# Strassen's scheme for one product of a four-layer graph network, with its norms put off and its Sturm counts taken from both ends

## The chip, the cores and the metric

The kernel runs on one core of one Trainium2 chip. The metric is the device time of the program in microseconds (us). Before the change it was 2614.92 us, the median of three runs (2614.4 to 2616.12).

## The reference

`x` is 128 graphs of 64 nodes with 256 features: 8192 rows of 256, all in fp32, and `adj` is one 64x64 matrix. Four layers follow each other, and each computes `x = layernorm(x + layer(x))`. Cut to what matters:

```python
# layer 0
A2 = adj * adj
h = relu(A2 @ (x @ W1))          # 256 -> 512
h = relu(A2 @ (h @ W2))          # 512 -> 1024
y = A2 @ (h @ W3)                # 1024 -> 256
# layer 1
L = normalized_laplacian(adj); _, U = eigh(L)
y = U @ (relu((U.T @ x) @ W1 + b1) @ W2 + b2)
# layer 2: two graph convolutions, then LSTMs over windows of 1, 2, 3, 4 nodes
# layer 3: graph attention
```

Layer 0 and the eigenvectors of one 64x64 matrix do not depend on each other; layer 1 needs both.

## The kernel before

The rows stand as 64 tiles of 128 (two graphs each) in `X` in SBUF for the whole run. There are two stages.

**Stage one** is layer 0 and, beside it, the eigenvectors. `layer0(g)` is a generator that works on 256 rows (two tiles) in five steps. `mixed` multiplies by the squared adjacency (`sqT2`, two graphs in one 128x128 block), which also brings the features onto the partitions; the product with W1 gives `h1`; `mixed` again gives `m2` (512 features in 4 chunks by 256 rows); the second product takes `m2` through W2 (`aw2`), 8 chunks of outputs with 4 matmuls of 128x256 each, and ScalarE (ACT) applies relu from PSUM into `h2`; the third product with W3 and a last product with `sqT2` give the layer's output. VectorE adds it to `X` (line 658) and `norm_parts` normalises (lines 472 to 485: statistics on VectorE, the power on GpSimd, the scaling on VectorE).

`eigen` is a second generator. It takes the 64x64 matrix to tridiagonal form in 62 steps (lines 140 to 196). Each step is one small matmul `pc` on TensorE (line 75) and some 25 small VectorE instructions on 64 partitions, of which line 163 writes the operand `LV` of the next matmul. Then Sturm counts find all 64 eigenvalues at once (lines 288 to 310): 6 passes with 16 trial points for each; each pass walks the 64 rows with a reciprocal and a multiply-add per row (lines 298 and 299), each depending on the one before. The rest (lines 313 to 454) makes the eigenvectors from recursions and transposes.

A planner puts the streams in order. It keeps `now`, a TensorE clock that each `mm` advances by a fixed cost, and each generator yields the time from which it may go on. The planner takes the first stream that is due, with `eigen` ahead of two groups of layer 0 (line 668 and following). `eigen` yields `after(n)`, which adds 0.21 us for each of n VectorE instructions to its own clock. In this stage TensorE and VectorE run their instructions exactly in the order in which the generators emit them (`manual_schedule`). PSUM is shared as 5 banks for layer 0 (`ps`) and 3 for `eigen` (`pa`, `pb`, `pc`).

**Stage two** is layers 1 to 3 on 16 groups of 512 rows, three groups in flight (`WAYS`), with a planner of its own for TensorE. `layer1` starts each group with `mixed` from `X`. The LSTM weights `wih` are loaded at the start of the kernel, `whh` when the first stage's pools close.

## Time and profile before

| | us |
|---|---|
| median of the runs | 2614.92 |
| profiled execution, own time | 2613.84 |
| its span | 2612.0 |
| TensorE busy | 2554.1 |
| VectorE busy | 1401.1 |
| ScalarE busy | 1048.5 |
| layer 0's last matmul starts | 923.51 |
| second stage's first matmul with X | 924.70 |
| last `LV` copy of the tridiagonal steps | 443.2 |
| first and last start of line 291 (Sturm passes) | 464.1, 690.1 |

The span is the time from the first to the last instruction in the trace; the execution's own time is 1.8 us longer. A row of the profile's groups names the line, the engine, the operation, what is written and read, the shape and the number; then the busy time, the mean of one in ns, and the idle time of that engine just before, with what ended it. A fp32 matmul is two instructions in the trace, so 64 rows of "128x256" are 32 matmuls of the source.

### The profile page before, as it was taken

The page shows a single profiled execution, that of the slowest core. Times are in us where ns is not written, and L with a number is a line of the kernel's source. Part 1 is how long each engine was busy: PE and PEld are TensorE (multiplying, and loading weights), DVE is VectorE, ACT ScalarE, POOL GpSimd, SP SyncE. Part 2 cuts the span into 40 slices and gives each one's busy share as a digit, 9 for nine tenths or more (in the row PEclk, how much of TensorE's full clock was granted, in tenths as well). Part 3 has the DMA queues.
Part 4 walks back from the last instruction along what each step waited for, and adds up shares of the span by engine and source line. Part 5 has one row for each costly group of instructions (what it writes and reads, how often), then busy time and mean ns, then how long its engine had stood idle before and what let it go on. Part 6 is the DMA issues. An engine that isn't in the chain of part 4 may idle for free.

```text
span 2612.0 us, 39806 instructions
## 1 busy us (share of the span) xinstructions
PE 2554.1 (98%) x15276; PEld 2240.8 (86%) x15276; DVE 1401.1 (54%) x5423; ACT 1048.5 (40%) x2599; POOL 132.2 (5%) x284
## 2 busy tenths in 40 slices
PE   8999999999999999999999999999999999999996
PEld 7888887888887889898899899898898998978994
DVE  5777777888864053434534544445445345353335
ACT  2232222222222234444544444544544444444444
POOL 0000000000000010000000000000000000000001
PEclk9999999999999999999999999999999999999998
DMA  8000000000000010000000000000000000000000
GB/s 278 1 1 1 1 1 1 1 1 1 1 1 1 1 49 1 9 1 9 9 1 9 9 1 9 7 4 9 1 9 9 1 9 9 1 9 1 1 2 25
DMA packets 24814, 32.19 MB, mean 12 GB/s; under 512 B 2352, under 2 KB 21552, under 8 KB 24624
## 3 DMA queue, kind: packets, MB, share of 16 engines
q1 hardware_dynamic: 24384, 29.60, 3.3%
q8 instruction: 120, 1.97, 0.3%
q14 instruction: 70, 0.57, 0.1%
q10 hardware_dynamic: 240, 0.05, 0.0%
HBM read 21.25 MB, written 8.39 MB: 11 GB/s over the span
## 4 chain that ended last, share of the span: by engine, by line
PE 87%; DVE 7%; ACT 3%; POOL 2%; issue 1%; DMA 0%; ACTq 0%; POOLq 0%; DVEq 0%
PE ps L607 84%; POOL ln_rs L475 1%; PE ps L720 1%; DVE X L485 1%; DVE ln_st L472 1%; PE ps L934 1%; DVE X L884 1%; PE pc L75 1%; ACT gates L821 1%; POOL ln_rs L474 1%; DVE ln_mv L473 0%; ACT L821 0%; ACT L947 0%; ACT att L947 0%; ACT w L876 0%
## 5 line engine op out<-in xcount | busy, mean ns | idle before, releaser
L607 PE MATMUL ps<-w,wih 128*128 128x128 f32 (+2 forms) x4992 | 895.5, 319 | 1.7 <-DVE w L840 1.7
L607 PEld LDWEIGHTS ps<-w,wih 128*128 128x128 f32 x4992 | 764.5, 191 | 51.3 <-issue 8.4
L821 ACT ACTIVATE gates<-ps,cbi 128x128 f32<-128x128 f32 (+2 forms) x1248 | 498.0, 409 | 568.0 <-PE ps L607 561.9
L607 PE MATMUL ps<-hs,whh 128*128 128x128 f32 (+2 forms) x3072 | 541.8, 304 | 7.9 <-DVE hs L831 7.6
L607 PEld LDWEIGHTS ps<-hs,whh 128*128 128x128 f32 x3072 | 454.4, 191 | 36.1 <-DVE hs L831 11.9
L607 PE MATMUL ps<-m,aw 128*128 128x256 f32 x2048 | 452.3, 380 | 0.0
L607 PEld LDWEIGHTS ps<-m,aw 128*128 128x128 f32 x2048 | 385.2, 190 | 50.2 <-issue 0.8
L615 ACT ACTIVATE h<-ps 128x256 f32<-128x256 f32 (+1 forms) x320 | 135.9, 425 | 393.6 <-PE ps L607 393.2
L607 PE MATMUL ps<-aw,h 128*128 128x256 f32 x1024 | 228.8, 380 | 0.0
L607 PEld LDWEIGHTS ps<-aw,h 128*128 128x128 f32 x1024 | 193.4, 190 | 36.5 <-issue 12.4
L826 DVE TENSOR_TENSOR gates<-gates 128x128 f32<-128x128 f32 (+2 forms) x256 | 89.1, 348 | 238.7 <-ACT gates L821 238.7
L474 POOL TENSOR_SCALAR ln_rs<-ln_mv 128x2 f32<-128x2 f32 x128 | 35.1, 274 | 2444.8 <-DVE ln_mv L473 2364.7
L829 ACT ACTIVATE gates<-c 128x128 f32<-128x128 f32 (+2 forms) x288 | 98.2, 341 | 114.0 <-DVE c L828 92.2
L485 DVE TENSOR_SCALAR X<-X,ln_mv,ln_rs 128x256 f32<-128x256 f32 x248 | 91.5, 409 | 96.7 <-POOL ln_rs L475 96.6
L840 DVE TENSOR_TENSOR w<-gates 128x256 f32<-128x256 f32 (+2 forms) x160 | 59.8, 379 | 130.4 <-PE ps L607 84.7
L825 DVE TENSOR_TENSOR c<-c,gates 128x128 f32<-128x128 f32 (+2 forms) x192 | 62.6, 326 | 117.5 <-ACT gates L821 115.3
L607 PE MATMUL ps<-aw,m 128*128 128x512 f32 x256 | 120.8, 595 | 0.0
L831 DVE TENSOR_TENSOR hs<-gates 128x128 f32<-128x128 f32 (+2 forms) x192 | 62.7, 328 | 101.9 <-ACT gates L829 52.9
L472 DVE BATCH_NORM_STATS2 ln_st<-X 128x6 f32<-128x256 f32 x256 | 99.0, 410 | 1.5
L298 DVE RECIPROCAL br<-Q 64x16 f32<-64x16 f32 x378 | 92.3, 244 | 12.5
L299 DVE SCALAR_TENSOR_TENSOR Q<-br,es,Q 64x16 f32<-64x16 f32 x378 | 85.8, 227 | 13.3
L475 POOL TENSOR_TENSOR ln_rs<-ln_rs,half 128x2 f32<-128x2 f32 x128 | 91.6, 716 | 10.0
(328 smaller groups left out, 2437.1 us busy)
## 6 DMA issues: line engine op xcount, KB each, us to landing
out_dram<-X SPq DMA_DIRECT2D x32, 256.0 KB, 2.1
X<-in_x_dram SPq DMA_DIRECT2D x31, 256.0 KB, 6.0
wih<-in_c_ih_dram SPq DMA_DIRECT2D x4, 1024.0 KB, 9.1
aw<-in_a_w_dram SPq DMA_DIRECT2D x3, 1024.0 KB, 9.9
whh<-in_c_hh_dram SPq DMA_DIRECT2D x3, 1024.0 KB, 5.5
aw<-in_a_w_dram SPq DMA_DIRECT2D x1, 512.0 KB, 4.6
cw<-in_c_w_dram SPq DMA_DIRECT2D x2, 256.0 KB, 3.5
X<-in_x_dram SPq DMA_DIRECT2D x2, 128.0 KB, 2.5
```

The source lines that it names most:

```text
L298: V.reciprocal(r, Q[:, k - 1, :])
L299: V.scalar_tensor_tensor(Q[:, k, :], r, es[:, 0, k:k + 1], Q[:, k, :], op0=ALU.mult, op1=ALU.add)
L472: nc.vector.bn_stats(st[:, t, :], x[:, t, :])
L475: nc.gpsimd.tensor_tensor(rs, rs, half[:, :n], ALU.pow)
L485: nc.vector.tensor_scalar(x[:, t, :], x[:, t, :], mv[:, t, 0:1], rs[:, t:t + 1], op0=ALU.subtract, op1=ALU.mult)
L607: PE.matmul(out, lhsT, rhs, start=start, stop=stop)
L615: S.activation(dst, src, AF.Relu)
L821: S.activation(gate[q][:, h, :], pp, AF.Tanh if q == "g" else AF.Sigmoid, bias=bias[:, j:j + 1])
L825: V.tensor_mul(c[:, h, :], c[:, h, :], gate["f"][:, h, :])
L826: V.tensor_mul(to, gate["i"][:, h, :], gate["g"][:, h, :])
L829: S.activation(gate["i"][:, h, :], c[:, h, :] if p > 1 else to, AF.Tanh)
L831: V.tensor_mul(new[:, h, :], gate["o"][:, h, :], gate["i"][:, h, :])
```

## The change

Layer 0 works on groups of 512 rows. Its second product is cut into 2x2 blocks: rows into two halves of 256, the 512 inputs into two halves, and the 1024 outputs into two halves. Winograd's form of Strassen's scheme makes the four blocks of the result with seven block products instead of eight. Four sums of blocks of `m2` (S1 to S4) are made on VectorE for every group, four sums of blocks of W2 (T1 to T4) once, in group 0. Each product is made in two parts (`j`), one PSUM bank each, and VectorE combines them (`u2`, `u3`, `join`), with relu on ACT from SBUF to SBUF afterwards.

The buffers of layer 0 become single (`pa` has bufs=1), groups wait for each other by name (`behind`), and PSUM is shared as 2 banks `ps`, 4 banks `prod`, 2 banks for `eigen` (`pb` is merged into `pa`). Only groups 0 to 2 are normalised in stage one; for the others, `group(g)` in stage two emits the norm ahead of `layer1`. `wih` is loaded when stage one closes, in turn with `whh`.

In `eigen`, the tridiagonal step loses one instruction: the small constant that line 151 added now stands in an extra column of `xr`. A step's due time is `after(30)` instead of `after(28)`. The Sturm counts run on 128 partitions: the lower 64 hold the matrix from its top, the upper 64 from its bottom, each half walks 32 rows, and the two join in the middle.

The diff, cut to its core:

```diff
     for i in range(N - 2):
-        V.tensor_scalar(rm, rest, 1e-30, None, op0=ALU.add)
-        V.tensor_scalar(ss, v0, v0, rm, op0=ALU.mult, op1=ALU.add)
+        V.tensor_scalar(ss, v0, v0, rest, op0=ALU.mult, op1=ALU.add)
...
-        yield after(28)
+        yield after(30)
...
+    HALF = N // 2
...
     for _ in range(PASSES):
...
-        for k in range(1, N):
-            r = sb([N, FAN], "br")
+        for k in range(1, HALF):
+            r = sb([W, FAN], "br")
             V.reciprocal(r, Q[:, k - 1, :])
-            V.scalar_tensor_tensor(Q[:, k, :], r, es[:, 0, k:k + 1], Q[:, k, :], op0=ALU.mult, op1=ALU.add)
+            V.scalar_tensor_tensor(Q[:, k, :], r, es2[:, k:k + 1], Q[:, k, :], op0=ALU.mult, op1=ALU.add)
             if k % 2:
                 yield after(7)
+        r = sb([W, FAN], "br")
+        V.reciprocal(r[:N, :], Q[:N, HALF - 1, :])
+        V.tensor_scalar(r[N:, :], r[:N, :], es[:, 0, HALF:HALF + 1], None, op0=ALU.mult)
+        V.tensor_add(Q[N:, HALF - 1, :], Q[N:, HALF - 1, :], r[N:, :])
...
-    pa = phase_a.enter_context(tc.tile_pool(name="pa", bufs=2))
+    pa = phase_a.enter_context(tc.tile_pool(name="pa", bufs=1))
...
-    wih = [load(keep, f"wih{i}", c_ih[i], "(k p) f -> p k f", [P, 2, 1024], p=P) for i in range(4)]
...
+    def behind(name, g):
+        while done[name] < g:
+            yield now[0] + 0.3
+
     def layer0(g):
-        xs = X[:, 2 * g:2 * g + 2, :]
+        xs = X[:, 4 * g:4 * g + 4, :]
...
+        if g == 0:
+            V.tensor_sub(T3, B22, B12)
+            V.tensor_sub(T1, B12, B11)
+            V.tensor_sub(T2, B22, T1)
+            V.tensor_sub(T4, T2, B21)
+        yield from behind("second", g - 1)
+        m2 = tl(pa, [P, 4, 512], "m2")
+        yield from mixed(m2, h1, 4, 1.4)
...
+        V.tensor_add(S1, A21, A22)
+        V.tensor_sub(S2, S1, A11)
+        V.tensor_sub(S3, A11, A21)
+        V.tensor_sub(S4, A12, S2)
...
-        for c in range(8):
-            p = tl(psa, [P, 512], "ps")
-            run(p[:, :2 * P], [(aw2[:, k, c * P:(c + 1) * P], m2[:, k, :]) for k in range(4)])
-            relu(h2[:, c, :], p[:, :2 * P])
-            yield now[0] + (1.3 if c == 7 else 0.0)
+        def product(w, a, j):
+            p = tl(psa, [P, 2, 256], "prod", bufs=4)
+            for i in range(2):
+                cols = slice((2 * j + i) * P, (2 * j + i + 1) * P)
+                run(p[:, i, :], [(w[:, k, cols], a[:, k, :]) for k in range(2)])
+            return p
...
+        def join(j, r, c, x, y, op=ALU.add):
+            V.tensor_tensor(quarter(j, r, c), x, y, op)
+            relu(quarter(j, r, c), quarter(j, r, c))
...
+            def six(p, p1=p1, u2=u2):
+                V.tensor_add(u2, p1, p)
+
+            def seven(p, u2=u2, u3=u3):
+                V.tensor_add(u3, u2, p)
+
+            def five(p, j=j, u2=u2, u3=u3):
+                join(j, 1, 1, u3, p)
+                V.tensor_add(u2, u2, p)
+
+            def four(p, j=j, u3=u3):
+                join(j, 1, 0, u3, p, ALU.subtract)
+
+            def three(p, j=j, u2=u2):
+                join(j, 0, 1, u2, p)
+
+            def two(p, j=j, p1=p1):
+                join(j, 0, 0, p1, p)
+
+            for then, w, a in ((one, B11, A11), (two, B21, A12), (six, T2, S2), (seven, T3, S3), (four, T4, A22),
+                               (five, T1, S1), (three, B22, S4)):
+                p = product(w, a, j)
+                if late:
+                    late[0](late[1])
+                late = then, p
...
                 yield now[0]
...
+        for t in (2, 0):
+            p = tl(psa, [P, 2, D], "ps", bufs=2)
+            mm(p, sqT2, s3[:, t:t + 2, :])
+            yield now[0] + 0.4
+            x2 = xs[:, t:t + 2, :]
+            V.tensor_add(x2, p, x2)
+            if g < WAYS:
+                rows_norm(tc, small, x2, half)
...
+    wih, whh = [], []
+    for i in range(4):
+        wih.append(load(wb, f"wih{i}", c_ih[i], "(k p) f -> p k f", [P, 2, 1024], p=P))
+        whh.append(load(wb, f"whh{i}", c_hh[i], "(k p) f -> p k f", [P, 2, 1024], p=P) if i else None)
...
     def group(g):
         xs = X[:, 4 * g:4 * g + 4, :]
-        ready = yield from layer1(xs)
+        ready = [0.0, 0.0]
+        if g >= WAYS:
+
+            ready = []
+            for t in range(0, 4, 2):
+                norm(xs, t, ready)
+        ready = yield from layer1(xs, ready)
```

The function that handles product `one` copies its bank to `p1` on ACT. Each product's additions are emitted after the next product's matmuls (`late`).

## The prediction

> **What bounds the kernel now.** I read the page's shares first, then the busy time of each engine by stage, then the timeline inside a stage. The page and its chain of waits say that TensorE sets the time:

> ```profile
> PE 2554.1 (98%) x15276; PEld 2240.8 (86%) x15276; DVE 1401.1 (54%) x5423; ACT 1048.5 (40%) x2599; POOL 132.2 (5%) x284
> ...
> PE 87%; DVE 7%; ACT 3%; POOL 2%; issue 1%; DMA 0%; ACTq 0%; POOLq 0%; DVEq 0%
> ```

> The 54% of VectorE is a mean over stages that differ. Busy time by stage, columns: stretch, its length, PE, PEld, DVE, ACT, POOL:

> ```profile
> 20.00:443.00 423.00, 419.19 (x2027) 347.69 (x2026) 324.60 (x1940) 123.13 (x373) 12.98 (x28) 1.00 0.09 29
> 443.00:464.00 21.00, 20.35 (x101) 16.01 (x100) 14.43 (x82) 4.95 (x12) 0.93 (x2) 1.00 0.00 1
> 464.00:738.00 274.00, 274.00 (x1289) 225.90 (x1288) 233.51 (x881) 70.00 (x168) 11.80 (x20) 1.00 0.00 1
> 738.00:812.00 74.00, 74.00 (x343) 60.47 (x342) 50.99 (x297) 17.25 (x42) 1.87 (x4) 1.00 0.00 1
> 812.00:924.50 112.50, 111.21 (x525) 91.05 (x524) 13.23 (x44) 27.56 (x66) 5.15 (x11) 1.00 0.06 20
> 924.50:2585.00 1660.50, 1630.28 (x10895) 1483.08 (x10893) 749.68 (x2121) 792.63 (x1911) 94.29 (x197) 1.00 0.02 6
> ```

> The rows are the tridiagonalisation, its clean-up, the Sturm counts, the rest of the eigenvectors, the end of layer 0, and the second stage. While the first four run, VectorE is busy 77%, 69%, 85% and 69% beside a full TensorE. That is the room into which the change puts additions. Timeline of one tridiagonal step (start, length, engine, line):

> ```profile
> 303.08 0.38 PE L75 MATMUL pc<-AQ,LV 128*128 128x128 f32 x2
> ...
> 303.50 0.23 DVE L175 SCALAR_TENSOR_TENSOR junk<-pc,q,xr 64x23 f32<-64x23 f32 x1 [1.88 <-PE pc L75]
> ...
> 305.02 0.14 DVE L151 TENSOR_SCALAR q<-q 64x1 f32<-64x1 f32 x1
> 305.20 0.26 DVE L152 TENSOR_SCALAR q<-xr,q 64x1 f32<-64x1 f32 x1
> ...
> 307.30 0.18 DVE L163 COPY LV<-u 64x64 f32<-64x64 f32 x1
> 307.41 0.67 DVE L658 TENSOR_TENSOR X<-ps,X 128x512 f32<-128x512 f32 x1
> ```

> From L175 to the end of L163 is 4.0 us, and L167 to L174 (300.28 to 301.61) came before it: 5.3 us of VectorE, in one piece, per step. 62 steps in 423 us are 6.8 us each. Two later rows:

> ```profile
> L298 DVE RECIPROCAL br<-Q 64x16 f32<-64x16 f32 x378 | 92.3, 244 | 12.5
> L299 DVE SCALAR_TENSOR_TENSOR Q<-br,es,Q 64x16 f32<-64x16 f32 x378 | 85.8, 227 | 13.3
> L658 DVE TENSOR_TENSOR X<-ps,X 128x512 f32<-128x512 f32 x32 | 21.9, 685 | 117.4 <-PE ps L607 117.3
> ```

> A Sturm pair is 0.54 us from start to start (621.77, 622.28, 622.82 in the timeline, about).

> [...] L658 shows 673 to 694 (median 691)[...]; every Strassen addition has this size. [...] L175 held VectorE 1.88 us for its small matmul, with nothing run in between. [...]

> **Removed: matmuls.** Per 512 rows the second product had 64 matmuls of 128x256; seven products of 8 are 56. Timeline: 32 such matmuls ran from 901.90 to the next start at 915.71, 0.432 us each. 16 groups x 8 x 0.432 = **-55 us** on TensorE, all on the path, since TensorE is full. The other matmuls keep number and size.

> **Added: VectorE work.** Per group 4 S and 14 U additions (18 x 0.70 with the gap = 12.6 us; the S read SBUF alone, where L757's 128x512 mean is 676 ns, so the price is bounded within 3%) and two output additions (1.4, as before). Sturm: 6 x 31 pairs instead of 6 x 63 saves 192 x 0.54 = 104 us, and the block work per pass shrinks from about 5.5 to 4.6 us. The step loses L151 (0.19 us): 5.1 us. In the compiled order the steps occupy 451 us of matmul time and the Sturm counts 151 us. Steps: 62 x 5.1 = 316, plus 8.8 groups x 14 = 123, plus 4 weight sums of 1024 elements (about 1.2 each, 5) and three groups' norms (12): 456 of 451. Sturm: 186 x 0.54 + 6 x 4.6 = 128, plus 2.95 x 14 = 169 of 151. **VectorE is full in both**, and it has no time to catch up.

> **Where TensorE then waits.** A step is queued on VectorE as one block ahead of the additions of the products issued after it. I follow the compiled order from one small matmul pc (time 0; a product is 4 x 0.432 = 1.73 us). The pattern repeats every 15 steps and two groups, about 7.2 us of matmuls per step.
> First group: the step falls just before product one. Its block ends at 4.2 (7 instructions need no pc and ran before it), S1 and S2 at 5.6; TensorE is through products one and two at 3.7: product six waits 1.9. Three steps on, the block ends at 5.5, the join of product four at 6.2 and its relu on ACT (0.6) at 7.0; the third matmul of the third product wants it at 4.6: 2.4. Three steps later the output addition stands behind a block until 4.9, and holds one of the two ps banks that TensorE wants at 1.6; with the relu before it 3.9. Sum 8.2.
> Second group: S falls under other work; four additions a step make 7.9 us of VectorE against 7.2, and the four prod banks run out by 0.5 and 1.3; the ps banks cost 0.4 and 2.0. Sum 4.2.
> 12.4 per 15 steps x 56/15 steps = **+46**. Group 0, with the weight sums in front of its S: **+5**. Sturm: the excess of 18 less what buffers hold, **+17** (three product phases; blocks are only two pairs long, so no long block). Clean-up and the last eigenvector blocks of up to 40 instructions (8 us): **+6**. Together +74. Bounds: if the queues even everything out, only the Sturm excess, 16; if every estimate is a third short, 100.

> **Moved: norms.** 13 groups x 4 tiles x (0.46 + 0.10 + 0.41) = 50 us of VectorE go to the second stage, and 26 POOL pairs of 0.93 us. VectorE is 45% busy there, TensorE idles 30 of 1660 us. A group now starts with a norm chain of about 5 us (two halves, POOL between) where it started at once; two other groups cover most of it. I take 0.9 us for each of 13: **+12**; at best 2, at worst 30, if every norm delays a recurrent cell on its queue too.

> **Moved: weight loads.** wih's 4 MB go from 43 us to the end of layer 0, ahead of whh on SP's queue; behind them stand only output stores, much later. 1 MB landed in 5.3 to 7.4 us, so seven take some 18 us at the 410 GB/s seen there; the first wih matmul came 38.5 us after the second stage began (962.99), whh 62 us. Cost 0; without that cover up to 18. Fewer ACT instructions (about 13 instead of 15 us per 512 rows), pb merged into pa (two copies waited for, once) and the longer due time of a step: 0.

> **Sum.** The profiled execution took 2613.84 (span 2612.0; the median of the runs is 2614.92): 2613.84 - 55 + 74 + 12 = **2645**.

> **Rivals.** (1) *The buffers absorb the bursts, faster.* Four prod banks hold 7 us of products and two groups are interleaved; VectorE needs some 750 us of layer 0's 861 us of matmuls. For it: before, TensorE lost only 4 us in 423 beside 77% busy VectorE. Against it: before, no matmul of layer 0 waited for VectorE except through X. With waits of 16 to 40 and the second stage at +8: 2583 to 2607, say 2600. It decides as soon as all waits stay under 38 us. Chance 0.22. (2) *Nothing measurable*: waits of 38 to 48, about 2614. 0.10. (3) *The norms cost most*: waits as forecast, but the second stage +35: 2668. 0.08. (4) *The eigenvectors end last*: their last copy stands 139 us of matmuls ahead of layer 0's end, so backlog delays TensorE with them and they can't be last; within the forecast's upper end.

> **Numbers.** Forecast 0.60 (2625 to 2680). Slower 0.68, same 0.10, faster 0.22; 0.2% (5 us) is about what a measurement can tell from no change. Range 2596 to 2680: it cuts the lower third of the faster case and the tail over 100 us of waits.

> **What would show it.** After: layer 0 ends near 943 (924.5 before), the last step's LV copy near 509, the last eigenvector copy near 803; TensorE idle in the steps about 11%, waiting for DVE ss, h2, u2 and X and ACT h2; VectorE over 90% busy in the steps and the counts; the last 110 us of layer 0 free of waits; the second stage about 1699 instead of 1687. If TensorE is over 95% busy during the steps, the block argument is wrong, and rival 1 holds. If wih or whh matmuls wait for a DMA, the cover failed.

## The result and the profile after

The changed kernel takes 2711.48 us (2710.94 to 2711.78, four runs) against 2614.68 for the kernel before on the same chip (four runs, of which the first three gave the 2614.92 above): a ratio of 1.0369 [1.0351, 1.0387]. It is slower, as forecast, but by 97 us where 30 were forecast, and it lies outside the range of 2596 to 2680. The profiled execution took 2711.31 us, its span is 2709.5. The page's shares and its chain of waits:

```profile
PE 2554.6 (94%) x15020; PEld 2214.9 (82%) x15020; DVE 1474.7 (54%) x5317; ACT 1039.2 (38%) x2407; POOL 126.8 (5%) x284
...
PE 71%; DVE 20%; POOL 3%; ACT 3%; issue 2%; DMA 0%; ACTq 0%; DVEq 0%; POOLq 0%
```

Two things are to be seen. VectorE's share of the chain rose from 7 to 20%. And TensorE is busy 2554.6 us, as before (2554.1), although it has 256 records fewer and 55 us of matmuls are gone: the matmuls that are left must have become slower. Busy time by stage (stretch, length, PE, PEld, DVE, ACT, POOL, granted clock, DMA share, GB/s) says where:

```profile
20.00:534.00 514.00, 466.70 (x2140) 369.31 (x2139) 397.18 (x1979) 132.17 (x308) 5.56 (x12) 0.97 0.05 16
555.00:733.00 178.00, 167.59 (x760) 134.38 (x758) 157.37 (x549) 39.46 (x66) 0.00 (x0) 0.98 0.00 1
733.00:812.00 79.00, 74.50 (x319) 57.97 (x320) 58.63 (x296) 17.72 (x30) 0.00 (x0) 0.97 0.00 1
812.00:967.50 155.50, 154.92 (x723) 125.29 (x723) 45.68 (x92) 37.51 (x62) 1.52 (x3) 0.99 0.04 15
967.50:2682.00 1714.50, 1648.95 (x10894) 1497.17 (x10894) 784.58 (x2271) 796.51 (x1911) 113.98 (x247) 0.99 0.02 8
```

The first row holds the tridiagonal steps, then come the Sturm counts, the rest of the eigenvectors, the end of layer 0 and the second stage. PE's column is now short of the length while the eigenvectors run, and the clock, 1.00 in every one of these stages before, is below it in all. Layer 0 ends at 967.34, where the next matmul starts (924.48 before): +42.9 us. The second stage, from there to the end of the span, takes 1742.2 us (1687.5): +54.6. (The 1741 in the expectations below counts from its first matmul with `X`.)

To separate waiting from slower matmuls I cut both traces into windows of 5 us and summed two things: TensorE's idle time, and (1 - granted clock) x length, called *clock lost* below.

| | idle before | idle after | clock lost before | clock lost after |
|---|---|---|---|---|
| stage one, from 20 us to layer 0's end | 5.8 | 65.0 | 0.0 | 23.8 |
| second stage, up to its last 27 us | 30.2 | 65.6 | 3.4 | 22.6 |

Clock lost counts the whole of a slow stretch, also the part in which TensorE is idle and loses nothing more. For the busy part alone it is 22.3 in stage one (0.0 before) and 18.1 in the second stage (2.9 before).

So the second stage has 35 us more of idle time and 15 more of lost clock, 50 of its 55. In stage one -55 (matmuls) + 59 + 22 gives +26 of +43. What remains, 5 and 17 us, has no record of its own. In part it comes from the trace, in which the ends of matmuls are modelled: at 314.33 (below) four records fill 1.03 us, while a run of them starts one every 0.22, so the pause after them seems 0.16 too short. Taken the same way, by the usual distance from start to start, this is 9 us at the 51 pauses of stage one, where 12 pauses before the change make 2; in the second stage it is 9 and 7. The rest, some 10 us in stage one and 3 in the second, stays open.

How the clock is lost, in TensorE's timeline of the steps (start, length, line, tiles, records; in brackets the idle time before and its releaser):

```profile
314.33 1.03 PE L633 MATMUL ps<-aw,h 128*128 128x256 f32 x4
317.46 2.86 PE L633 MATMUL ps<-aw,h 128*128 128x256 f32 x12 [2.10 <-ACT h L641]
...
336.20 1.12 PE L633 MATMUL ps<-s,sqT 128*128 128x512 f32 x2 [0.47 <-ACT h L641]
340.26 6.69 PE L633 MATMUL ps<-aw,m 128*128 128x512 f32 x8 [2.94 <-DVE X L768]
```

The wait of 2.10 us costs 2.10: the 12 records after it run at their usual pace. The wait of 2.94 us costs twice: the 8 records after it take 6.69 us, where 8 of this shape take 3.60 (381.52 in the trace of experiment *gaps*), and the granted clock is 0.50 meanwhile (columns as in the table by stage):

```profile
339.48:346.31 6.83, 6.05 (x7) 2.53 (x8) 2.44 (x11) 0.60 (x1) 0.00 (x0) 0.50 0.00 0
```

There are 11 such slow stretches in stage one, of 3.41 to 10.24 us, and half of their length is the 23.8 us of lost clock. VectorE in the same moments:

```profile
335.77 0.24 DVE L179 SCALAR_TENSOR_TENSOR junk<-pc,q,xr 64x27 f32<-64x27 f32 x1 [2.96 <-PE pc L76]
...
339.42 0.19 DVE L167 COPY LV<-u 64x64 f32<-64x64 f32 x1
339.53 1.27 DVE L768 TENSOR_TENSOR X<-ps,X 128x512 f32<-128x512 f32 x2
```

VectorE itself waited 2.96 us for `pc`, then ran the step in one piece, 335.77 to 339.6. The two output additions (L768) stood behind it: the product of the first was through at 333.70 (`ps<-s,sqT`, 1.02 us from 332.68), and the addition ran 5.8 us later, at 339.53. Their ps banks stayed full, and TensorE waited. That is the mechanism of the forecast, with the lost clock as its second half.

TensorE's waits in the second stage, first of the kernel before, then after (us in total, times, longest):

```profile
PE ps L607 <- DVE hs L831: 7.6, 7, 1.5
PE ps L607 <- DVE X L485: 3.0, 2, 2.1
```

```profile
PE ps L633 <- DVE hs L944: 24.1, 8, 4.6
PE ps L633 <- DVE X L512: 9.0, 5, 6.9
```

The recurrent product of the LSTMs waits for its state `hs`. VectorE ahead of one such wait:

```profile
1557.78 0.17 DVE L500 BATCH_NORM_AGGREGATE ln_mv<-ln_st 128x2 f32<-128x6 f32 x1
...
1559.81 0.73 DVE L512 TENSOR_SCALAR X<-X,ln_mv,ln_rs 128x256 f32<-128x256 f32 x2 [0.82 <-POOL ln_rs L502]
...
1562.88 0.32 DVE L939 TENSOR_TENSOR c<-gates 128x168 f32<-128x168 f32 x1
...
1564.42 0.41 DVE L512 TENSOR_SCALAR X<-X,ln_mv,ln_rs 128x256 f32<-128x256 f32 x1 [0.91 <-POOL ln_rs L502]
...
1565.67 0.57 DVE L944 TENSOR_TENSOR hs<-gates 128x168 f32<-128x168 f32 x2
```

In TensorE's timeline, first one of these products before the change, then after:

```profile
1008.40 1.30 PE L607 MATMUL ps<-hs,whh 128*128 128x168 f32 x8
```

```profile
1566.05 2.61 PE L633 MATMUL ps<-hs,whh 128*128 128x168 f32 x8 [4.62 <-DVE hs L944]
```

Norms of two groups stand together on VectorE's queue (statistics L500, scaling L512), each half with a wait of 0.8 for GpSimd inside it. The cell's instructions (L939, L944) come between and behind them. The same wait of 4.62 stands at 1780.78, 1995.67 and 2210.62. The 8 records after it take 2.61; before, 8 such records took 1.30. The waits for `hs` grew by 16.5 us and those for `X` by some 8, of which one alone is 6.9.

### The profile page after: what moved, and what is told of

Read it like the earlier page. It is cut to its first block, busy times and chain, and to the rows that moved or that the text cites. A ratio compares the mean times of both kernels' runs of the same rounds, so it can differ in the third digit from the quotient of the medians.

```text
span 2709.5 us, 39051 instructions
## 1 busy us (share of the span) xinstructions
PE 2554.6 (94%) x15020; PEld 2214.9 (82%) x15020; DVE 1474.7 (54%) x5317; ACT 1039.2 (38%) x2407; POOL 126.8 (5%) x284
## 3 DMA queue, kind: packets, MB, share of 16 engines
q8 instruction: 118, 1.93, 0.3%
## 4 chain that ended last, share of the span: by engine, by line
PE 71%; DVE 20%; POOL 3%; ACT 3%; issue 2%; DMA 0%; ACTq 0%; DVEq 0%; POOLq 0%
PE ps L633 63%; PE prod L633 5%; POOL ln_rs L502 2%; DVE X L512 2%; DVE ln_st L499 2%; PE ps L833 1%; DVE h L710 1%; DVE br L317 1%; DVE Q L318 1%; POOL ln_rs L501 1%; DVE ln_mv L500 1%; ACT gates L934 1%; PE ps L1047 1%; DVE X L997 1%; DVE u L723 0%
## 5 line engine op out<-in xcount | busy, mean ns | idle before, releaser
L633 PE MATMUL ps<-hs,whh 128*128 128x128 f32 (+2 forms) x3072 | 548.5, 306 | 24.5 <-DVE hs L944 24.1
L633 PE MATMUL ps<-aw,h 128*128 128x256 f32 x1024 | 236.3, 390 | 19.8 <-ACT h L641 19.8
L939 DVE TENSOR_TENSOR gates<-gates 128x128 f32<-128x128 f32 (+2 forms) x256 | 89.2, 348 | 248.9 <-ACT gates L934 248.9
L641 ACT ACTIVATE h<-h 128x512 f32<-128x512 f32 x128 | 80.2, 630 | 268.3 <-DVE h L710 268.1
L512 DVE TENSOR_SCALAR X<-X,ln_mv,ln_rs 128x256 f32<-128x256 f32 x248 | 91.9, 410 | 109.7 <-POOL ln_rs L502 109.7
L633 PE MATMUL ps<-aw,m 128*128 128x512 f32 x256 | 133.4, 653 | 17.7 <-DVE X L768 14.5
L633 PE MATMUL prod<-ss,tw 128*128 128x256 f32 x512 | 117.4, 381 | 10.3 <-DVE ss L693 10.3
L633 PE MATMUL prod<-ss,aw 128*128 128x256 f32 x512 | 117.9, 381 | 6.5 <-DVE u L723 3.8
L633 PEld LDWEIGHTS ps<-aw,m 128*128 128x128 f32 x256 | 49.1, 205 | 83.4 <-issue 40.1
L633 PE MATMUL prod<-m,aw 128*128 128x256 f32 x512 | 117.1, 380 | 0.0
L501 POOL TENSOR_SCALAR ln_rs<-ln_mv 128x2 f32<-128x2 f32 x128 | 30.7, 240 | 1838.5 <-DVE ln_mv L500 1837.0
L633 PEld LDWEIGHTS prod<-ss,tw 128*128 128x128 f32 x512 | 95.8, 190 | 25.3 <-DVE ss L693 12.3
L944 DVE TENSOR_TENSOR hs<-gates 128x128 f32<-128x128 f32 (+2 forms) x192 | 62.0, 327 | 99.4 <-ACT gates L942 57.9
L633 PEld LDWEIGHTS prod<-ss,aw 128*128 128x128 f32 x512 | 95.8, 190 | 22.2 <-PE prod L633 4.8
```

The costliest lines, as they stand in the source:

```text
L501: nc.gpsimd.tensor_scalar(rs, mv[:, :, 1], EPS, None, op0=ALU.add)
L512: nc.vector.tensor_scalar(x[:, t, :], x[:, t, :], mv[:, t, 0:1], rs[:, t:t + 1], op0=ALU.subtract, op1=ALU.mult)
L633: PE.matmul(out, lhsT, rhs, start=start, stop=stop)
L641: S.activation(dst, src, AF.Relu)
L939: V.tensor_mul(to, gate["i"][:, h, :], gate["g"][:, h, :])
L944: V.tensor_mul(new[:, h, :], gate["o"][:, h, :], gate["i"][:, h, :])
```

## The experiments

Theory: small VectorE work of another stream, in long pieces on an in-order queue, makes TensorE wait, and the longer waits also cost clock. Rivals: single buffers and two `ps` banks make the waits; the new Sturm counts are at fault; the slow matmuls have nothing to do with the waits. Each run is compared by its ratio to runs of the kernel before on its own chip (medians 2616.76, 2617.31 and 2615.81 for experiments 1 to 4, 5 to 8, 9 and 10).

**1. norms_back: all norms in stage one again.**

```diff
-            if g < WAYS:
-                rows_norm(tc, small, x2, half)
+            rows_norm(tc, small, x2, half)
...
-        if g >= WAYS:
...
-                norm(xs, t, ready)
```

> The put-off of the norms alone is undone: all 16 groups are normalised in the first stage. Theory (the put-off norms stand on VectorE ahead of recurrent cells, and the clock of TensorE falls after the long waits that this makes): the second stage goes back from 1741 us to 1687, within 6, and has no stretch with a granted clock under 0.9 but the one before (near the end of the groups). The first stage, where VectorE is full, gets longer by 5 to 40 us: total 2662 to 2700. Rival (the second stage is slower because the weight loads and the buffers moved): the second stage stays within 10 us of 1741, total 2715 to 2755.

2682.02 us, ratio 1.0252 [1.0222, 1.0282]. The second stage takes 1691 us, 51 less than with the change and within 4 of before; its clock lost falls from 22.6 to 5.1. Layer 0 ends at 988.98, 22 later. So nearly all of the second stage's +55 is the put-off norms, and putting them off loses about 29 in total: they cost more there than beside the eigenvectors.

**2. no_eigen: the change without the eigenvectors.**

```diff
-    eig = [0.0, eigen(tc, phase_a, a64, ident, eig_c, u2, ut2, now)]
+    eig = None
+    V.memset(u2, 0.0)
+    V.memset(ut2, 0.0)
```

> The changed kernel without the eigenvectors (they are left out and read as zeros, so layer 1 adds only biases). Theory (TensorE's waits in layer 0 come from eigen's blocks on VectorE): layer 0 ends at 840 to 855, which is its matmul time of 835 plus the start, with under 10 us idle and full clock; total 2582 to 2598. Rival (single buffers and only two ps banks make the waits, whatever eigen does): layer 0 ends after 880, total over 2620.

2591.76 us; layer 0 ends at 848.57. Busy time from 20 to 848 us:

```profile
20.00:848.00 828.00, 827.98 (x3861) 675.22 (x3860) 224.85 (x358) 208.62 (x346) 7.08 (x15) 1.00 0.04 12
```

TensorE isn't idle at all and the clock is 1.00. Strassen's scheme with single buffers and two `ps` banks therefore makes no wait of its own; the rival falls in this form. All of stage one's idle time and lost clock comes from running beside `eigen`. Whether deeper buffers would have taken up what `eigen` does to VectorE was not tried. The second stage stays at 1741.

**3. before_eigen: the kernel before, with the changed eigenvectors.** Only `eigen` (one instruction less in a step, Sturm counts from both ends, `after(30)`) is replaced in the kernel before.

> The kernel before with eigen's part of the change alone (Sturm counts from both ends, one instruction less in a step, due time 30). Theory (TensorE is full there and VectorE's idle time is worth nothing): 2614 within 5, eigenvectors done some 90 us earlier than 812. Rival (the counts over 128 partitions or the later due time disturb the order): over 2620.

2618.21 us (18 runs), ratio 1.0006 [0.9999, 1.0014]; layer 0 ends at 928.41. The last transposes of the eigenvectors come at 707.4 instead of 820.2, earlier than expected. The new eigenvectors alone cost nothing that can be measured, and gain nothing: beside the old layer 0 they were under a full TensorE anyway.

**4. gaps: the clock by itself.** In the kernel before, without eigenvectors, VectorE work of 0 to 7 additions is put ahead of one product in each of 24 groups.

```diff
-        S.copy(s3, p)
-        yield now[0] + 1.5
+        V.tensor_copy(s3, p)
+        for _ in range(g % 8 if 4 <= g < 28 else 0):
+            V.tensor_add(s3, s3, gap0)
```

> A measurement of the clock by itself: the kernel before without the eigenvectors (left out, read as zeros); in groups 4 to 27 of layer 0 the output product waits for a chain on VectorE of a copy and 0 to 7 additions of zero of 0.7 us, so that TensorE stands still for about 0.9 to 5.8 us, three times each. Theory (TensorE's clock falls after a wait of more than some 2.5 us): waits under 2 us cost their own length; after waits over 3 us the next matmuls take about double for 2 to 4 us, so each costs 1.5 to 2 us more than its length, and the granted clock is under 0.8 there. Rival (the low clock of the changed kernel has nothing to do with waits): the matmuls after each wait take what they take elsewhere, and each wait costs its own length.

The 2.5 us of the theory lies between the wait of 2.10 us and that of 2.94 us in the timeline of the steps. 2704.95 us (one run); idle 86.1, clock lost 30.7 in stage one. The product after the wait is two records that take 1.12 us at full clock:

```profile
353.07 1.13 PE L607 MATMUL ps<-s,sqT 128*128 128x512 f32 x2 [2.23 <-DVE s L658]
354.04 1.95 PE L607 MATMUL ps<-sqT,h 128*128 128x128 f32 x16
...
380.56 1.12 PE L607 MATMUL ps<-s,sqT 128*128 128x512 f32 x2 [2.96 <-DVE s L658]
381.52 3.60 PE L607 MATMUL ps<-aw,m 128*128 128x512 f32 x8
...
415.64 1.14 PE L607 MATMUL ps<-s,sqT 128*128 128x512 f32 x2 [3.69 <-DVE s L658]
416.60 3.58 PE L607 MATMUL ps<-sqT,h 128*128 128x128 f32 x16
...
446.21 2.08 PE L607 MATMUL ps<-s,sqT 128*128 128x512 f32 x2 [4.42 <-DVE s L658]
...
638.99 2.08 PE L607 MATMUL ps<-s,sqT 128*128 128x512 f32 x2 [2.96 <-DVE s L658]
```

| wait, us | length of the two records after it, us |
|---|---|
| 0.78, 1.51, 2.23 | 1.12 to 1.13 in every case |
| 2.96 | 1.12, 2.08, 2.08 |
| 3.69 | 1.13, 1.14, 1.58 |
| 4.42 | 2.08, 2.08, 1.45 |
| 5.14, 5.87 | 2.08 in all six |

The slow matmuls come with the length of the wait, with no eigenvectors and no Strassen near. The first to be slow is mostly the one that ends the wait; after the second wait of 3.69 us it is the next ones, 16 records in 3.58 us, where they took 1.95 at 354.04. So of the six waits of 2.96 and 3.69 us four cost clock and two do not, and all nine of 4.41 us and more do. A slow stretch lasts 3.41 or 6.83 us and so costs at most 1.7 or 3.4 us.

What decides between the two cases stands in the same trace. The clock changed in it only at moments that lie whole multiples of 3.41 us apart. Cut into windows on this grid, the first and the second wait of 2.96 us look so (columns as above):

```profile
375.67:379.08 3.41, 1.93 (x9) 1.34 (x8) 1.38 (x2) 0.00 (x0) 0.00 (x0) 1.00 0.00 0
379.08:382.49 3.41, 1.93 (x5) 0.98 (x6) 2.12 (x4) 0.00 (x0) 0.00 (x0) 1.00 0.00 0
635.08:638.49 3.41, 0.95 (x5) 0.50 (x3) 2.32 (x4) 0.00 (x0) 0.00 (x0) 1.00 0.00 0
638.49:641.90 3.41, 2.91 (x4) 1.36 (x5) 1.21 (x3) 0.00 (x0) 0.00 (x0) 0.50 0.00 0
```

The first wait is shared out between two windows, and TensorE is busy 1.93 us in each. The second falls for the most part into one, which is left with 0.95 us; the next window gets half the clock. The twelve traces of this document, cut in the same way up to 2570 us, hold 8803 windows at full clock. Half the clock followed on 105 of the 106 in which TensorE was busy under 43%, on 5 of the 38 with 43 to 51%, and on none of the 8659 with more. From these counts comes an estimate, with 43% as the limit: a wait that takes 57% of a window, 1.9 us, can cost clock, and one of 3.9 us always does, since it can't be shared out so that both windows stay under that.

**5. stretch: thinner eigenvectors.**

```diff
-        yield after(30)
+        yield after(37)
...
-                yield after(7)
+                yield after(9)
```

> The changed kernel with later due times for eigen (37 instead of 30 for a step, 9 instead of 7 for two Sturm pairs), so that its VectorE work is spread over 850 us of layer 0's 861 us of matmuls instead of 722. Theory (VectorE is full during the steps and the counts): waits fall by a third to two thirds, layer 0 ends at 905 to 945 instead of 968, total 2650 to 2690. If only the length of a step's block makes the waits, not how full VectorE is: the same waits per step, layer 0 ends within 15 us of 968.

2665.08 us, ratio 1.0182 [1.0153, 1.0212]; layer 0 ends at 921.24. Idle 34.2 and clock lost 10.2 in stage one: both fall to about half, inside the third to two thirds expected, and with steps and counts further apart the stage now ends 3 us earlier than before the change. A step's piece is as long as with the change, so its length alone does not set the waits: how closely the pieces follow each other counts too. In the steps VectorE is busy 74% instead of 77%, and TensorE idles 28 us instead of 47.

**6. split: a step in three pieces.** Same instructions, in pieces of some 12, 9 and 9 with layer 0's work let in between.

```diff
+        yield after(9)
         V.tensor_scalar(g0, rest, 1.5e-30, -1.0, op0=ALU.is_gt, op1=ALU.mult)
...
-        yield after(30)
+        yield after(9)
...
         xr = nx
+        yield after(12)
```

> The changed kernel with each tridiagonal step's block of VectorE instructions emitted in three pieces (due times 12, 9 and 9 in place of 30), so that additions of layer 0 can stand between them; eigen ends at the same place in the order. Theory of the block (an addition behind a block holds up a bank or the third product): the waits for ACT h2 and for X in the steps at least halve, layer 0 ends at 935 to 955, total 2675 to 2700. If VectorE is merely full, the order of its instructions is worth nothing: layer 0 ends within 10 us of 968.

2674.77 us, ratio 1.0219 [1.019, 1.0249]; layer 0 ends at 929.21, 38 us earlier than with the change and a little better than expected. TensorE's waits in stage one, with the change and with this:

```profile
PE ps L633 <- ACT h L641: 29.1, 22, 3.7
PE ps L633 <- DVE X L768: 16.5, 9, 3.2
PE prod L633 <- DVE ss L693: 10.3, 5, 3.1
```

```profile
PE pc L76 <- DVE LV L168: 15.1, 16, 4.4
PE ps L635 <- ACT h L643: 14.4, 11, 3.7
PE ps L635 <- DVE X L770: 8.3, 9, 2.5
```

The waits for `h` and `X` halve, and the one for the sums S (`ss`) is gone. The amount of VectorE work is the same; only its grain and the due times that go with it changed, and 38 us went. VectorE is busier in the steps than with the change (82% of 479 us, where it was 77% of 514), so its share does not set the waits either. A new wait came in: the small matmul `pc` now comes too early for its step (15.1).

**7. spread: the put-off norms in single pieces.** The norms of group g+3 are cut into statistics and scaling, and one piece is emitted at each call of `lstm` of group g.

```diff
+            if chores.get(g):
+                next(chores[g].pop(0), None)
             ready = yield from lstm(hT, p, first, nw)
...
-                norm(xs, t, ready)
+                parts = norm_parts(tc, small, nxt[:, t:t + 2, :], half)
+                chores.setdefault(g, []).extend([parts, parts])
```

> The changed kernel with the put-off norms of group g+3 emitted while group g is in its recurrent cells, statistics and scaling at different calls, so that no start of a group waits for them. Theory (the norms cost because three sets of them stand in one piece on VectorE ahead of a cell, and because a group's first product no longer fills TensorE at that moment): the second stage takes 1688 to 1702 us instead of 1741, without a granted clock under 0.9 in mid-stage; total 2657 to 2674. Rival (50 us of VectorE more in a stage that is 45% busy cost their time wherever they stand): 1725 or more.

2677.0 us, ratio 1.0228 [1.0198, 1.0257]. The second stage takes 1707 us, 35 less than with the change, though 5 more than I expected at most, and the total is 3 over; clock lost is 8.6. The same norms in the same stage cost 19 (1707 against 1687.5) instead of 55, by their place on the queue.

**8. all3: 5, 6 and 7 together** (pieces after 14, 11 and 12 instructions, Sturm `after(9)`, norms spread).

> The three edits together (blocks in three pieces with due times of 14, 11 and 12, Sturm pairs at 9, norms spread in the second stage). If the waits have these three causes: layer 0 ends at 880 to 910, the second stage takes 1688 to 1702, total 2570 to 2614, faster than both kernels. If something else holds layer 0 (single buffers, two ps banks): it ends after 920 and the total is over 2615.

2606.06 us (2605.79 to 2606.66, four runs), ratio 0.996 [0.994, 0.9979]: 0.4% faster than the kernel before. Layer 0 ends at 901.59 and the second stage takes 1703, one more than expected at most. Busy time by stage:

```profile
20.00:900.00 880.00, 858.17 (x4028) 694.48 (x4027) 668.28 (x2982) 229.90 (x473) 7.07 (x15) 1.00 0.04 12
900.00:2577.00 1677.00, 1637.03 (x10898) 1482.93 (x10896) 785.73 (x2272) 791.31 (x1912) 117.01 (x246) 1.00 0.03 9
```

VectorE does what it does with the change (668 us against 675 in stage one, 786 against 785 after it), and 105 us are gone. The amount of work was not the fault.

**9. filler: more matmuls in place of the wait.** In the second stage, ten matmuls whose result nobody reads, ahead of groups 7, 9, 11 and 13.

```diff
+            if g in (7, 9, 11, 13):
+                idle = ps4()
+                for _ in range(10):
+                    PE.matmul(idle[:, :D], ident, dw[:, 0, :], start=True, stop=True)
```

> The changed kernel with ten matmuls of 128x256 more (4.4 us of TensorE, results not used) in each of the groups 7, 9, 11 and 13, at the start of the second stage's group, some 5 us ahead of the matmul that stands still 4.6 us for a cell's result in the changed kernel. They add 17.5 us of matmuls. Theory (the wait is set by VectorE, and what follows it runs at half clock because TensorE stood still): the four waits shrink to under 1.5 us, the clock stays at 1.00 there, and the total falls by 6 to 12 us, to 2699 to 2706. If the clock has nothing to do with standing still: the matmuls only fill the wait, 2709 to 2713. If the wait is not set by VectorE: up to 17 us more, 2715 to 2729.

2700.33 us (2699.46 to 2701.93), ratio 1.0323 [1.0307, 1.0338] where the change has 1.0369 [1.0351, 1.0387]. TensorE's timeline at the place of the wait shown above:

```profile
1555.81 4.48 PE L1095 MATMUL ps<-dw,ident 128*128 128x256 f32 x20
...
1567.03 0.55 PE L633 MATMUL ps<-hs,whh 128*128 128x168 f32 x2 [0.40 <-DVE hs L944]
```

TensorE has about 17.5 us more to do and ends 11 us earlier. The four waits of 4.62 are about 0.4, and clock lost in the stage falls from 22.6 to 10.5. Idle time falls by 17 us, as much as was added, so the gain is the clock: here a wait filled with useless work is cheaper than the wait.

**10. best: all3, with the third product in the order in which its inputs are made.**

```diff
-                    for c in range(k, k + 4):
+                    for c in ((0, 1, 4, 5), (2, 3, 6, 7))[k // 4]:
```

> The three edits together, and in the third product the four chunks of h2 that the first part (j = 0) of the second product makes are taken before the four of the second part, which puts 0.86 us more of matmuls ahead of each chunk that comes last from VectorE and ACT. The waits for ACT h2 (23.5 us in the three edits together) should fall by 6 to 14 us: layer 0 ends at 888 to 897 instead of 902, total 2592 to 2601. If those waits are set by how full VectorE is, the total stays within 3 us of 2606.

2605.86 us (2603.66 to 2606.59, five runs), ratio 0.9959 [0.9945, 0.9973]. Layer 0 ends 3 us earlier (898.64), but the time is not to be told from all3's. The wait that it was to shorten is unchanged in both rows that show it, and the two rows are the same in all3:

```profile
PEld ps L635 <- ACT h L643: 23.5, 33, 2.1
...
PE ps L635 <- ACT h L643: 3.8, 6, 1.2
```

The 23.5 us are waits of the weight loads (PEld), most of which passed beside running matmuls: the matmuls themselves waited only 3.8 us for `h` in all3 (`h1` and `h2` together, since names lose their numbers here), so there were no 6 to 14 us to be gained. What this wait was worth is read from PE's row and not from PEld's.

## Why the prediction was wrong in size

Two of the steps that make up its sum failed: waits were charged at their own length, without a term for the slower matmuls after them (37 us, 22 in stage one and 15 in the second), and the norms were taken to be covered (35 us of idle time where 12 were charged). By its own steps:

- **Matmuls -55: right.** At their usual distance from start to start the matmuls of stage one, those of `eigen` included, add up to 905 us before and 850 after. no_eigen, whose layer 0 keeps TensorE full, ended it at 848.57, inside the 840 to 855 us worked out with this term.
- **Waits of the first stage +74: right in mechanism, near in size.** Measured are 59 us of idle time, and some 66 with what the modelled ends hide. The steps were to lose 51 (46, and 5 for group 0): their idle time is 47 us of 514, against 4 of 423 before. The Sturm counts were to lose 17: 10, with 3 of clock. Clean-up and the last blocks +6: 2 and 5. no_eigen shows that the waits come from `eigen`, split that the length of its pieces makes them, and stretch that their distance does too.
- **Step that failed in stage one: each wait was charged at its own length.** The sum has no term for the matmuls after a wait. That term is 22 us. It was to be seen in the profile of before, where TensorE's timeline shows 4 records of one shape before and after two waits that lie close together:

```profile
2312.92 1.03 PE L607 MATMUL ps<-w,wih 128*128 128x256 f32 x4
...
2318.99 1.16 PE L607 MATMUL ps<-adT,X 128*128 128x128 f32 x8 [2.14 <-DVE X L485]
2321.14 2.08 PE L607 MATMUL ps<-ut,v 128*128 128x128 f32 x8 [0.99 <-ACT v L615]
2323.01 1.91 PE L607 MATMUL ps<-w,wih 128*128 128x256 f32 x4
```

1.03 became 1.91. Cut on this trace's grid:

```profile
2316.60:2320.01 3.41, 1.27 (x11) 1.02 (x9) 2.50 (x8) 0.78 (x2) 1.27 (x2) 1.00 0.00 0
2320.01:2326.84 6.83, 5.84 (x19) 4.90 (x18) 1.11 (x3) 2.08 (x5) 0.00 (x0) 0.50 0.00 0
```

The wait of 0.99 is not the cause: the clock fell at 2320.01, before that wait began, after a window in which TensorE was busy 1.27 us, with the wait of 2.14 in it. I had read the granted clock only by stages, where one such place in 1660 us still shows as 1.00. In this trace as in that of gaps, the clock granted after such a window is 0.50, and the matmuls take about double (1.91 for 1.03 here, 2.08 for 1.12 in gaps). The windows lie on a grid of 3.41 us in both, so the same wait can hit or miss. TensorE need not be wholly idle in one: 1.27 us of matmuls in 3.41 us (here) and 0.95 us (gaps) did not keep the clock up. With waits of 1.9 to 3.9 us in my own pattern, the question had to be asked.
- **VectorE "over 90% busy" in the steps and counts: wrong.** It is 77% and 88%. The price of an addition held: medians of 677 to 692 ns, where L658 before had 691. So did that of the four weight sums of 1024 elements: 1.209 to 1.225 us (L681 to L684), where about 1.2 was taken. But the step's 5.1 us were taken as occupied time, of which it is busy 4.6, and in the steps VectorE itself waits 72 us for `pc` (2.96 at the place above). The two engines wait for each other by turns, and neither is full. The forecast got the waits from following the pieces, and that was near; that VectorE had no time to catch up was wrong, though stretch shows that more time helps.
- **Norms +12: the larger miss.** Measured 55 in the second stage; norms_back gives 51 of it to the norms. The step that failed is "two other groups cover most of it", 0.9 us for each norm. The start of a norm's own group is covered in the main (waits for `X` grew by 8 us, 6.9 of them in one wait); the recurrent cells of the other groups, queued behind it on VectorE, are not (waits for `hs` grew by 16.5). The text named this as its worst case at 30 and rival 3 at 35, and that price is the idle time measured (35). Another 15 are clock: waits of 4.6 us are of a length that in gaps was followed by slow matmuls every time.
- **Weight loads 0: right.** No matmul of the second stage waits for a DMA.
- **Ends of the streams:** layer 0 was to end at 943 and ended at 967, the last `LV` copy at 509 and came at 534.6. The first is 24 late and the second 26. The clock explains most of it: 24 are lost at most in the whole stage, 17 of them by the end of the steps. The eigenvectors, forecast for 803, end at 829, still 138 us ahead of layer 0's end, as the text on rival 4 said.
- **Rival 1** (buffers absorb the bursts) falls with 65 us of idle time, and rival 2 with it. Rival 3 had the right place for the larger part of the miss.

Together: forecast +31 against the profiled execution, measured +97. The first stage missed 24 (43 against 19): 22 of clock and 10 that stay open, less 8 by which the waits fell short of 74. The second missed 43 (55 against 12): 23 of idle time, 15 of clock and 5 without a record.

## What to carry to other kernels

When a change puts small work of one stream in front of another stream's work on an engine that takes its queue in order (the first L768 above ran 5.8 us after its product), cost it by the length of the pieces and by how closely they follow each other, and not by the engine's share: the same VectorE work took 105 us less once it was cut and spread (all3). Price a TensorE wait by its length plus what the matmuls after it lose (at most 1.7 or 3.4 us in gaps), and ask first how busy it leaves TensorE in a window of 3.41 us: half the clock followed on 105 of 106 windows under 43%, on 5 of 38 with 43 to 51% and on none with more, and in gaps a wait of 2.96 us cost no clock where two windows shared it. Work moved out of a crowded stage costs what stands behind it on its queue in the new one: the put-off norms cost 55 us with recurrent cells behind whole norms, and 19 in single pieces (spread).
